# Cross-attention with residual: two heads' exponentials in one tile, two block transposes a quad instead of four

## The chip, the cores and the metric

The kernel runs on one core of a Trainium2 chip. The metric is the device time of one execution in microseconds. Before the change it is 595.76 us, the median of three runs (595.75 to 595.84).

## What is computed

For eight batches of 256 rows by 1024 columns, `x` is layer-normed, multiplied with `Wq` and split into 32 heads of 32 columns. Keys and values are both `ctx_4096` (256 rows a batch), split in the same way. Each head takes the softmax of its 256x256 scores and multiplies the result with the values; the heads are joined, multiplied with `Wout`, and `x` is added. All is fp32.

```python
x = (hidden_states - mu) * jax.lax.rsqrt(var + LN_EPS) * ln_gamma + ln_beta
Q = _split_heads(x @ Wq.T); K = _split_heads(memory_keys); V = _split_heads(memory_values)
scores = jnp.einsum('bhsd,bhtd->bhst', Q, K) * scale
probs = jax.nn.softmax(jnp.where(mask, scores, -jnp.inf), axis=-1)
attn = jnp.einsum('bhst,bhtd->bhsd', probs, V)
return residual + attn.transpose(0, 2, 1, 3).reshape(B, S, HIDDEN) @ Wout.T
```

## The kernel before, in words

**The quad.** The unit of work is a quad: four heads of one batch, which fill the 128 rows of one chunk of Q. There are eight quads a batch and 64 in all, numbered n. One loop runs over n, and the code is issued in the order in which each engine works it off; no scheduler reorders it. In turn n the loop issues, for TensorE: the scores of quad n+1 (`scores`, L362, 16 matmuls into four PSUM banks, one a head), the products of probabilities and values of quad n-2 (`values`, L492), steps of the output projection of the last batch (`product_steps`, L549), the next chunk of Q (`make_q`, L319), and further steps of the projection. For the other engines it issues the softmax of quad n+1 (`softmax_parts`).

**The softmax of one quad.** For each head j, `exps(j)` works on two halves of 128 rows by 256 scores. VectorE (DVE) copies the scores from PSUM to SBUF with the mask added and takes the row's minimum in the same instruction (L396; Q was multiplied with a negative scale); ScalarE (ACT) takes the exponential and sums the row (L400). Then `normalize(j)`: VectorE takes the reciprocal of the two sums (L407), and GpSimd (POOL) multiplies the two halves by it, in place (L409). Then `blocks(j)`: VectorE transposes the head's 128x512 values in blocks of 32x32 into a part of `pT` (L415). `aside` copies a half of `pT` for two heads to `pc` (ScalarE, L421). When all four heads are through, four DMAs on SyncE's queue (L472, L476) exchange blocks of 32 rows between partitions, which ends the transposition. The values of that quad are computed two turns later.

**The order on VectorE.** Within a quad it is: exps 0, 1, 2, reciprocal 0, exps 3, reciprocal 1, transpose 0, reciprocal 2, transpose 1, reciprocal 3, transpose 2, and transpose 3 in `tail()`. In the first nine quads (n up to `NQ`) the tail of a quad is issued behind exps 0 of the next quad; later it follows at once. Into this order other VectorE work is put: `hooks[0]` stands ahead of reciprocal 1 and `hooks[1]` behind transpose 0; a hook is the evacuation of a projection's PSUM bank (`keep`, L561, and `store`, L569). `fill` is a list of pieces of layer norm work of the first quads, of which one piece each was put behind reciprocals 1, 2 and 3 (batch statistics L211, the block transpose L290 of x, `ln_norm`, copies of x's transposes L284). After the quad come the batch statistics (L211 to L216), whose result `ve` GpSimd turns into `rstd` (L217), or the block transposes of x (L290), and GpSimd's sums for the projection (`sum_at`, L539), sums of weights (`sum_wo`, L177), residual additions (`add_res`, L565) and, in the first batch, the folding of gamma into the weights (`fold`, L341 and L342).

**The projection** takes seven products instead of eight per batch, with sums of the operands made by GpSimd. It has one PSUM bank, `po`, so a new product can begin, or go on after a partial result has been taken, only when VectorE or ScalarE has evacuated the bank. `STEPS` sets how many of its 28 steps stand in each turn, ahead of and behind `make_q`. In the last batch, for which no further Q is made, `make_q` falls out and the evacuation is issued ahead of the softmax.

**Buffers.** The pool `ep` of exponentials has four tiles of 128x512, one a head; `ptp` has three `pT`, `ps_s` four banks of scores.

Of the kernel before, what the change touches and what calls it, by code (L numbers as in the profile page):

```python
# [46 lines left out]
F32 = mybir.dt.float32  # L47
# [4 lines left out]
P = 128  # L52
# [7 lines left out]
def xattn_kernel(  # L60
# [13 lines left out]
    T = mask.shape[2]  # L74
# [4 lines left out]
    NS = S // P  # L79
    NT = T // P  # L80
    NO = D // 512
    K = 32
# [11 lines left out]
    vp = ctx.enter_context(tc.tile_pool(name="vp", bufs=2))  # L94
    qp = ctx.enter_context(tc.tile_pool(name="qp", bufs=8))
    atp = ctx.enter_context(tc.tile_pool(name="atp", bufs=2))
    ep = ctx.enter_context(tc.tile_pool(name="ep", bufs=4))
    ptp = ctx.enter_context(tc.tile_pool(name="ptp", bufs=3))
    asp = ctx.enter_context(tc.tile_pool(name="asp", bufs=3))
    up = ctx.enter_context(tc.tile_pool(name="up", bufs=1))  # L100
# [222 lines left out]
    def copy_q(n):  # L323
        b, o = divmod(n, NQ)
        q = qs[n] = qp.tile([P, S + 1], F32, tag="q", name=f"q_{n}")
        if b == 0:
            nc.scalar.activation(q, pqs.pop(n), AF.Copy, scale=NEG_SCALE)  # L327
        elif b == 1:
            nc.scalar.activation(
                q[:, :S], pqs.pop(n), AF.Identity, scale=NEG_SCALE, bias=qb[:, o : o + 1],  # L330
            )
        else:
            nc.scalar.activation(  # L333
                q[:, :S].rearrange("p (s a k) -> p a s k", s=NS, a=NA),
                pqs.pop(n).rearrange("p (a s k) -> p a s k", s=NS, a=NA),
                AF.Identity, scale=NEG_SCALE, bias=qb[:, o : o + 1],
            )
# [29 lines left out]
    def softmax(*args):  # L367
        for _ in softmax_parts(*args):
            pass
# [3 lines left out]
    def softmax_parts(n, new_q=(), between=(), hooks={}, fill=()):  # L373

        fill = list(fill)

        def fill_in():  # L380
            if fill:
                fill.pop(0)()

        pss = scs[n]
        pT = pTs[n] = ptp.tile([P, 2, NI, NH, NS, K], F32, tag="pT", name=f"pT_{n}")
        pc = asp.tile([P, NI, NH, NS, K], F32, tag="pc", name=f"pc_{n}")
        es, mns, dens = {}, {}, {}

        def exps(j, part=range(NS)):
            if 0 in part:  # L390
                es[j] = ep.tile([P, NS, T], F32, tag="e", name=f"e_{n}_{j}")
                mns[j] = sm.tile([P, NS], F32, tag="mn", name=f"mn_{n}_{j}")
                dens[j] = sm.tile([P, NS], F32, tag="den", name=f"den_{n}_{j}")
            e, mn, den = es[j], mns[j], dens[j]
            for s in part:
                nc.vector.tensor_tensor_reduce(  # L396
                    out=e[:, s, :], in0=pss[j][:, s, :], in1=mbs[n // NQ], scale=1.0,
                    scalar=NO_SCORE, op0=ALU.add, op1=ALU.min, accum_out=mn[:, s : s + 1],
                )
                nc.scalar.activation(  # L400
                    e[:, s, :], e[:, s, :], AF.Exp, bias=mn[:, s : s + 1], scale=-1.0,
                    accum_out=den[:, s : s + 1],
                )

        def normalize(j):
            rden = sm.tile([P, NS], F32, tag="rden", name=f"rden_{n}_{j}")
            nc.vector.reciprocal(rden, dens[j])  # L407
            for s in range(NS):
                nc.gpsimd.tensor_scalar(  # L409
                    es[j][:, s, :], es[j][:, s, :], rden[:, s : s + 1], 1.0,  # L410
                    ALU.mult, ALU.mult,
                )

        def blocks(j):
            nc.vector.transpose(  # L415
                pT[:, :, :, j, :, :].rearrange("p a i s k -> p (a i) s k"),
                es[j].rearrange("p s (b t) -> p b s t", t=K),
            )

        def aside(j):  # L420
            nc.scalar.copy(pc[:, :, ts(j, 2)], pT[:, 1, :, ts(j, 2)])  # L421

        if n == 0:
            for j in range(NH - 1):
                exps(j, (0,))
            yield
            exps(NH - 1, (0,))
            fill_in()
            yield
            for j in range(NH):  # L430
                exps(j, (1,))
            normalize(0)
            fill_in()
        else:
            exps(0)
            while tails:
                tails.pop()()
            for done in list(pvs):
                copy_at(done)
            exps(1)  # L440
            exps(2)
            normalize(0)
            exps(3)
        if n <= NQ:
            for q in new_q:
                copy_q(q)
        for hook in hooks.get(0, ()):
            hook()
        normalize(1)
        fill_in()  # L450
        blocks(0)
        for hook in hooks.get(1, ()):
            hook()
        normalize(2)
        fill_in()
        blocks(1)
        aside(0)
        normalize(3)
        fill_in()
        blocks(2)  # L460
        while fill:
            fill_in()
        if n > NQ:
            for q in new_q:
                copy_q(q)

        def tail():
            blocks(3)
            aside(1)

            for r in range(2):
                nc.sync.dma_start(pT[ts(2 * r, K), 1], pT[ts(2 * r + 1, K), 0])  # L472
            for load in between:
                load()
            for r in range(2):
                nc.sync.dma_start(pT[ts(2 * r + 1, K), 0], pc[ts(2 * r, K)])  # L476

        if n < NQ:
            tails.append(tail)
        else:  # L480
            tail()
        yield
# [16 lines left out]
    def copy_at(n):  # L499
        b, c = divmod(n, NQ)  # L500
        if c == 0:
            ats[b] = atp.tile([P, NC, NS, NA, K], F32, tag="at", name=f"at_{b}")
        for r, pv in enumerate(pvs.pop(n)):
            nc.scalar.copy(  # L504
                ats[b][:, c, :, ts(r, 2), :], pv.rearrange("p a s k -> p s a k")
            )
# [86 lines left out]
    for n in range(N):  # L593
        k = min(BATCH0[n] if n < NQ else 1, N - made)
# [56 lines left out]
    for c in range(NC):  # L651
        copy_x0(1, c, nc.scalar if c < NC // 2 else nc.vector)
    first = softmax_parts(0, (1,), (), {}, [
        partial(ln_stats, 1, 0), partial(ln_stats, 1, 1),
        partial(ln_norm, 1, 0, nc.vector), partial(ln_norm, 1, 1, nc.scalar),
# [14 lines left out]
    for n in range(N):  # L670
        b, i = divmod(n - NQ, NQ)
# [6 lines left out]
        if b >= 0 and i in (0, 1, 3, 4):  # L678
            s, h = {0: (0, 0), 1: (1, 0), 3: (1, 1), 4: (0, 1)}[i]
# [147 lines left out]
```

## Time and profile before

| | |
|---|---|
| time before, median of three runs | 595.76 us |
| profiled execution, its own time | 596.43 us |
| its span | 594.6 us |
| L415 transposes of 128x512 | 256, mean 709 ns, 181.4 us busy |
| L409 normalizations of 128x256 | 512, mean 481 ns, 237.3 us busy |
| L396 scores to SBUF with minimum | 512, mean 417 ns, 185.4 us busy |
| L400 exponentials | 512, mean 502 ns, 254.3 us busy |
| L290 transposes of 128x1024 (of x) | 12, mean 1206 ns, 14.5 us busy |
| VectorE waiting for scores (L396 on L362) | 33.5 us |
| VectorE waiting for GpSimd ahead of a transpose | 48.2 us |
| GpSimd waiting for a reciprocal ahead of L409 | 168.7 us |

The profile is of one execution. A row names the line of the kernel, the engine, the operation, the tiles written and read and their shapes, then busy time and mean duration. Where a row has an idle time, it is that of the engine ahead of these instructions, with what ended most of it. Timeline rows begin with the start and the duration in us, and end with the engine's idle time ahead of them where there was some. [...]

### The profile page before, as it was taken

What the parts mean: (1) busy time and instruction counts of PE and PEld (TensorE: products, weight loads), DVE (VectorE), ACT (ScalarE), POOL (GpSimd) and SP (SyncE); (2) the same over time, 40 slices, a digit from 0 to 9 for tenths busy, and PEclk for the clock granted to TensorE, in tenths of its full rate; (3) what the DMA queues carried; (4) which work ended last, traced back from release to release, by engine and by line L of the source; (5) the groups of instructions that cost most, each with busy time, mean ns of one, the idle gap of its engine ahead of it and who ended that gap; (6) DMA issues with size and microseconds to landing.
All of it is one profiled execution on the core that took longest, in us unless ns stands there. A gap on an engine that the chain in (4) does not pass through costs nothing.

```text
span 594.6 us, 18914 instructions
## 1 busy us (share of the span) xinstructions
PE 582.0 (98%) x6680; PEld 389.3 (65%) x6680; DVE 458.3 (77%) x1675; ACT 407.0 (68%) x1380; POOL 347.5 (58%) x630
## 2 busy tenths in 40 slices
PE   9999999999999999999999999999999999999997
PEld 8787776666666676666676667666666667654443
DVE  5878888697887878788787887878787677779801
ACT  4788786776777776686676876677677677667700
POOL 1568896987557644755447653484556564385600
PEclk9999999999999999999999999999999999999999
DMA  8566798545863667544674457654556355466541
GB/s 309 222 165 210 227 255 234 156 114 172 228 185 90 175 177 209 167 113 139 195 225 128 130 157 191 193 155 136 158 145 194 99 162 142 125 181 174 165 126 71
DMA packets 42063, 101.13 MB, mean 170 GB/s; under 512 B 8560, under 2 KB 8560, under 8 KB 41968
## 3 DMA queue, kind: packets, MB, share of 16 engines
q1 hardware_dynamic: 41680, 99.91, 57.4%
q8 instruction: 53, 0.87, 0.7%
q14 instruction: 42, 0.34, 0.2%
q10 hardware_dynamic: 288, 0.01, 0.0%
HBM read 51.65 MB, written 8.39 MB: 101 GB/s over the span
## 4 chain that ended last, share of the span: by engine, by line
PE 76%; POOL 12%; DVE 5%; issue 2%; DMA 2%; ACT 2%; SPq 1%; POOLq 0%; DVEq 0%; ACTq 0%
PE pq L319 29%; PE po_S L549 17%; PE sc L362 9%; PE pv L492 9%; POOL e L409 8%; PE po_A L549 7%; PE po L577 3%; DVE e L396 2%; POOL wo L177 2%; POOL wq L342 1%; PE busy L118 1%; DMA pT<-pc 1%; DVE pT L415 1%; DVE st L211 1%; DMA v<-in_kv_dram 1%
## 5 line engine op out<-in xcount | busy, mean ns | idle before, releaser
L409 POOL TENSOR_SCALAR e<-e,rden 128x256 f32<-128x256 f32 x512 | 237.3, 481 | 172.3 <-DVE rden L407 168.7
L400 ACT ACTIVATE e<-e,mn 128x256 f32<-128x256 f32 x512 | 254.3, 502 | 55.2 <-DVE mn L396 55.2
L319 PE MATMUL pq<-xnT,wq 128*128 128x256 f32 (+1 forms) x1008 | 230.7, 382 | 1.3 <-ACT q L327 1.2
L415 DVE STREAM_TRANSPOSE pT<-e 128x512 f32<-128x512 f32 x256 | 181.4, 709 | 55.4 <-POOL e L409 48.2
L319 PEld LDWEIGHTS pq<-xnT,wq 128*128 128x128 f32 x1008 | 188.9, 190 | 45.1 <-issue 17.9
L396 DVE CUSTOM_DVE_ANT_0 e<-sc,mb 128x256 f32<-128x256 f32 x512 | 185.4, 417 | 33.8 <-PE sc L362 33.5
L421 ACT COPY pc<-pT 128x512 f32<-128x512 f32 x128 | 79.2, 619 | 76.1 <-DVE pT L415 45.3
L549 PE MATMUL po_S<-wo,at 128*128 128x512 f32 x224 | 107.0, 603 | 3.3 <-DVE u L561 1.3
L400 ACT ACTIVATION_READ_ACCUMULATOR e<-e,mn 128x1 f32 x512 | 98.4, 192 | 0.0
L492 PE MATMUL pv<-pT,v 64*32 64x128 f32 x4096 | 74.6, 274 | 2.2 <-DMA pT<-pc 1.4
L362 PEld LDWEIGHTS sc<-k,q 32*128 32x128 f32 x1024 | 46.4, 184 | 46.3 <-issue 23.4
L362 PE MATMUL sc<-k,q 32*128 32x256 f32 x1024 | 74.3, 401 | 0.1
L492 PEld LDWEIGHTS pv<-pT,v 64*32 64x32 f32 x4096 | 57.3, 105 | 25.0 <-issue 12.9
L549 PEld LDWEIGHTS po_S<-wo,at 128*128 128x128 f32 x224 | 40.6, 189 | 38.8 <-issue 31.8
L549 PE MATMUL po_A<-wo,at 128*128 128x512 f32 x112 | 52.0, 598 | 0.0
L407 DVE RECIPROCAL rden<-den 128x2 f32<-128x2 f32 x256 | 39.3, 153 | 9.0 <-ACT e L400 6.3
L396 DVE DVE_READ_ACCUMULATOR2_ANT mn<- 128x1 f32 x512 | 42.7, 83 | 0.0
L549 PEld LDWEIGHTS po_A<-wo,at 128*128 128x128 f32 x112 | 20.8, 190 | 19.1 <-issue 18.4
L217 POOL TENSOR_TENSOR rstd<-ve,mhalf 128x1 f32<-128x1 f32 x16 | 9.4, 585 | 38.8 <-DVE ve L216 38.2
L504 ACT COPY at<-pv 128x128 f32<-128x128 f32 x128 | 26.1, 253 | 8.1 <-PE pv L492 8.1
L333 ACT ACTIVATE q<-pq,qb 128x256 f32<-128x256 f32 x48 | 22.6, 470 | 10.2 <-PE pq L319 10.2
L549 PE MATMUL po_S<-wo,s 128*128 128x512 f32 x56 | 26.9, 605 | 0.6 <-DVE r L569 0.6
(52 smaller groups left out, 299.7 us busy)
## 6 DMA issues: line engine op xcount, KB each, us to landing
v<-in_kv_dram SPq DMA_DIRECT2D x32, 512.0 KB, 4.3
pT<-pT SPq DMA_DIRECT2D x128, 128.0 KB, 2.3
pT<-pc SPq DMA_DIRECT2D x128, 128.0 KB, 3.9
k<-in_kv_dram SPq DMA_DIRECT2D x32, 256.0 KB, 3.4
x<-in_x_dram SPq DMA_DIRECT2D x14, 512.0 KB, 5.6
r<-in_x_dram SPq DMA_DIRECT2D x28, 256.0 KB, 4.4
out_dram<-r SPq DMA_DIRECT2D x28, 256.0 KB, 3.1
xnT<-xe SPq DMA_DIRECT2D x96, 64.0 KB, 3.1
```

Of the source, the lines that this page charges most:

```text
L319: nc.tensor.matmul(pqs[n], wq[:, o, c, :], xnTs[b](c), start=(c == 0), stop=(c == NC - 1),)
L333: nc.scalar.activation(q[:, :S].rearrange("p (s a k) -> p a s k", s=NS, a=NA), pqs.pop(n).rearrange("p (a s k) -> p a s k", s=NS, a=NA), A ...
L362: nc.tensor.matmul(scs[n][j][:, s, :], qs[n][r, ts(s, P)], ks[n - n % 2][r, n % 2, :], start=True, stop=True,)
L396: nc.vector.tensor_tensor_reduce(out=e[:, s, :], in0=pss[j][:, s, :], in1=mbs[n // NQ], scale=1.0, scalar=NO_SCORE, op0=ALU.add, op1=ALU.m ...
L400: nc.scalar.activation(e[:, s, :], e[:, s, :], AF.Exp, bias=mn[:, s : s + 1], scale=-1.0, accum_out=den[:, s : s + 1],)
L407: nc.vector.reciprocal(rden, dens[j])
L409: nc.gpsimd.tensor_scalar(es[j][:, s, :], es[j][:, s, :], rden[:, s : s + 1], 1.0, ALU.mult, ALU.mult,)
L415: nc.vector.transpose(pT[:, :, :, j, :, :].rearrange("p a i s k -> p (a i) s k"), es[j].rearrange("p s (b t) -> p b s t", t=K),)
L421: nc.scalar.copy(pc[:, :, ts(j, 2)], pT[:, 1, :, ts(j, 2)])
L492: nc.tensor.matmul(pvs[n][r][j * HD : (j + 1) * HD], vs[n - n % 2][ts(r, 2 * K), i, ds(n % 2 * P + j * HD, HD)], pT[ts(r, 2 * K), :, i, j, ...
L504: nc.scalar.copy(ats[b][:, c, :, ts(r, 2), :], pv.rearrange("p a s k -> p s a k"))
L549: nc.tensor.matmul(pos[b], operand(b, name)[:, c], wo[:, which, c], start=begins and c == 0, stop=c == NK - 1, skip_group_check=not begins,)
```

## The change

The exponentials of heads 0 and 1 share one tile of 128x1024, and those of heads 2 and 3 another; the pool has two of these instead of four of half the size. `blocks` transposes such a pair with one instruction, and is called twice a quad: `blocks(0)` behind reciprocal 2, `blocks(1)` in the tail. The two calls between reciprocals fall out, and with them two of the places where a piece of `fill` was issued: after the first piece, what is left of `fill` is issued behind reciprocal 3. `hooks[1]` now stands between reciprocals 1 and 2, ahead of the first transpose.

```diff
-    ep = ctx.enter_context(tc.tile_pool(name="ep", bufs=4))
+    ep = ctx.enter_context(tc.tile_pool(name="ep", bufs=2))
...
-        es, mns, dens = {}, {}, {}
+        eps, es, mns, dens = {}, {}, {}, {}
...
-                es[j] = ep.tile([P, NS, T], F32, tag="e", name=f"e_{n}_{j}")
+                if j % 2 == 0:
+                    eps[j // 2] = ep.tile([P, 2, NS, T], F32, tag="e", name=f"e_{n}_{j}")
+                es[j] = eps[j // 2][:, j % 2]
...
         def blocks(j):
             nc.vector.transpose(
-                pT[:, :, :, j, :, :].rearrange("p a i s k -> p (a i) s k"),
-                es[j].rearrange("p s (b t) -> p b s t", t=K),
+                pT[:, :, :, ts(j, 2)].rearrange("p a i j s k -> p (a i) (j s) k"),
+                eps[j].rearrange("p j s (b t) -> p b (j s) t", t=K),
             )
...
         normalize(1)
         fill_in()
-        blocks(0)
         for hook in hooks.get(1, ()):
             hook()
         normalize(2)
-        fill_in()
-        blocks(1)
+        blocks(0)
         aside(0)
         normalize(3)
-        fill_in()
-        blocks(2)
         while fill:
             fill_in()
...
         def tail():
-            blocks(3)
+            blocks(1)
             aside(1)
```

## The prediction

> **What bounds the kernel now.** I read the page's busy shares first, then the stretches, then VectorE's waits, then single quads. The page says that TensorE is never idle for long:
>
> ```profile
> PE 582.0 (98%) x6680; PEld 389.3 (65%) x6680; DVE 458.3 (77%) x1675; ACT 407.0 (68%) x1380; POOL 347.5 (58%) x630
> L409 POOL TENSOR_SCALAR e<-e,rden 128x256 f32<-128x256 f32 x512 | 237.3, 481 | 172.3 <-DVE rden L407 168.7
> L415 DVE STREAM_TRANSPOSE pT<-e 128x512 f32<-128x512 f32 x256 | 181.4, 709 | 55.4 <-POOL e L409 48.2
> ```
>
> Only 12.6 us of the span are idle on TensorE, so relieving VectorE can win little; the question is whether it gets worse. Busy time by stretch (columns: length, then PE, PEld, DVE, ACT, POOL) shows three regimes:
>
> ```profile
> 15.00:125.00 110.00, 106.07 (x1246) 78.81 (x1245) 90.91 (x349) 85.25 (x286) 88.74 (x148) 1.00 0.67 201
> 125.00:527.00 402.00, 401.88 (x4659) 268.35 (x4661) 321.70 (x1173) 285.97 (x974) 231.58 (x428) 1.00 0.56 161
> 527.00:565.00 38.00, 34.51 (x514) 17.60 (x506) 33.91 (x126) 28.24 (x102) 25.18 (x46) 1.00 0.63 182
> ```
>
> TensorE is full in the middle; at the beginning and from 527 us on it waits. In the chain that ended last, those two stretches run through the normalization (POOL e, L409) and VectorE, the middle through TensorE.
>
> I call a quad's exponentials X0 to X3 (L396/L400), its reciprocals R0 to R3 (L407), normalizations N0 to N3 (L409, two instructions each), transposes T0 to T3 (L415). One quad of the last stretch, from the timeline:
>
> ```profile
> 544.62 0.16 DVE L407 RECIPROCAL rden<-den 128x2 f32<-128x2 f32 x1
> 544.87 3.81 POOL L409 TENSOR_SCALAR e<-e,rden 128x256 f32<-128x256 f32 x8 [3.56 <-DVE rden L407]
> 546.75 0.71 DVE L415 STREAM_TRANSPOSE pT<-e 128x512 f32<-128x512 f32 x1
> 547.48 0.17 DVE L407 RECIPROCAL rden<-den 128x2 f32<-128x2 f32 x1
> 547.72 0.71 DVE L415 STREAM_TRANSPOSE pT<-e 128x512 f32<-128x512 f32 x1
> 548.71 0.71 DVE L415 STREAM_TRANSPOSE pT<-e 128x512 f32<-128x512 f32 x1 [0.27 <-POOL e L409]
> 549.35 0.65 DVE L569 TENSOR_TENSOR r<-po_S,r 128x512 f32<-128x512 f32 x1
> 550.05 3.70 PE L549 MATMUL po_S<-wo,s 128*128 128x512 f32 x8 [0.65 <-DVE r L569]
> ```
>
> R0 releases GpSimd, which normalizes eight times without a gap (3.81 us): R3 at 547.48, behind T1, is just in time for N3 at 547.74. N3 ends at 548.68, T3 starts, then the evacuation, and TensorE's next products wait for that. The loop returns every 7.37 us (T3 at 541.35, 548.71).
>
> [...] the kernel already transposes 128x1024 at L290, twelve times, in 1.203 us, against 2 x 0.709 = 1.418. [...]
>
> **The change, part by part.**
>
> Removed and added: 256 transposes of 0.709 us become 128 of, by the L290 row, 1.203: 181.4 to 154 us busy. What counts is start to start: T3 at 340.25 to the next instruction at 340.89 is 0.64; L290 at 332.37 to the next at 333.50 is 1.13. Two became one: 1.28 to 1.13, so 0.3 us saved a quad, 19 us in all, under a full TensorE. The new access pattern isn't in the trace; bounds are one short transpose (0.71) and two (1.42). I take L290's 1.20, as its row has the same element count and minimum and median agree.
>
> Moved: VectorE's order was R1 T0 R2 T1 R3 T2 T3. It is R1 R2 TA R3 TB. TA holds heads 0 and 1 and so waits for N1; R3 is behind TA; N3 waits for R3. TB needs N3.
>
> (a) R3. In a quad as above, N1 ends at 546.72; TA runs from 546.75, R3 follows at 547.89 and takes 0.12, GpSimd starts 0.1 later: N3 at 548.11 instead of 547.74, +0.37. Where GpSimd had been behind (N1 ends 69.66: R3 would come at 70.83, N3 at 71.05, not 70.58) it is +0.47. GpSimd stands still meanwhile.
> (b) TB starts when N3 ends, as T3 did, but holds VectorE for 1.13, not 0.64: +0.5.
> Sum: +0.87 (GpSimd behind: +0.97) before VectorE may go on. Behind TB stand the evacuations, batch statistics, the block transpose of x and the next quad's X0; the ScalarE copy (L421) too.
> (c) Where an evacuation stood between T0 and R2 (three slots in eight), it now stands ahead of TA, and the gap of 0.53 that it made ahead of N2 (L409 x4 ends 337.84, next 338.37) goes: only +0.42 there, and the evacuation comes 0.8 earlier in its quad.
>
> Queues: TensorE's and SP's orders don't change; buffers of e hold as many bytes, and X2 waits only for the last quad's TB, ahead of it on the same engine. In the first quads three pieces of filling work move behind R3: ln_norm's shift (POOL), its x (ACT, 1.24 us) and the second copy of x's transposes.
>
> **Last stretch.** Nothing covers the loop. Five T3s (533.98, 541.35, 548.71, 556.07, 563.44), each 0.87 later: 4.4 us. The work from 565 on is 25.96 of 29.6 us of TensorE, behind them: +4.4.
>
> **Middle.** Per batch of eight slots, from one start of X0 (the rows of 306 to 377 us) to the moment VectorE is free for the next, against the start of the next scores:
> slot 1: needs 8.39, TensorE gives 8.39; 2: 8.99, 9.26; 3: 8.99, 8.39; 4: 8.52, 9.25; 5: 7.95, 8.38; 6: 7.28, 9.25; 7: 7.41, 8.39; 0: 8.49, 9.27.
> Sums: 66.0 of 70.6. The cover is the 4.6 us that VectorE waits for scores in a batch. Added: 0.88 in slots 0, 1, 7; 0.97 in 2; 0.90 in 3; 0.42 in 4, 5, 6: 5.8. It now needs 71.8, 1.2 more than TensorE. VectorE may be late by what its readers leave: in slot 2 the sums on GpSimd, started by ve (L216), end at 319.92 for products at 320.68; in slot 4 the evacuation has some 2 us. After those, each of the four full batches (16th to 47th quad) costs 1.2: +4.8. The batch from quad 48 has no layer norm and waits of 1.2 to 2.4 us a slot: covered.
>
> **Beginning.** Step by step from 12 us: the moved x delays q (L327 24.47) to 25.35: TensorE +0.9. Quads 3 and 4 end +0.6 later each, the next gains a little as its x transposes stop holding R2: +1.9 at scores 66.9. Then GpSimd is the bound (N's, wo 1.25, qb, wq 1.85: a cycle of 6.87): +0.47 per quad by (a), and where ve follows TB, +0.97. From N0 at 67.82 (+1.1, part of the delay being absorbed) I get +1.65, +2.2, +2.95, +3.9, then the sums at 104.2 and TensorE's products at 108.27 by +4.85. Up to the evacuation at 126.54, which gains by (c): +5.3 at 127.3.
>
> Sum: 5.3 + 4.8 + 4.4 = 14.5. The span of 594.6 becomes 609.1; with the 1.8 around it (profiled execution 596.43) 610.9. The median of the runs is 0.7 under the profiled one: 595.76 + 14.5 = **610.3**.
>
> **Rivals.**
> - B: the middle is covered after all. Its excess is 1.2 us of 70.6; errors of 0.15 a slot remove it. Beginning and end remain: +9.7, 605.5. If the beginning is half absorbed too, 603. For it: lateness may spare the ScalarE waits (L407 on e: 6.3).
> - C: the middle is worse. The same error the other way doubles the excess: +4.8, and late copies (L421) may cost the beginning more: 615.
> - D: no change. VectorE only sheds work under a full TensorE, and all lateness is covered: 595.8. Against it: the products at 550.05 wait for the evacuation behind T3, with no cover to use.
> - E: faster. If the long transpose costs hardly more than a short one (below some 0.75 us, where (a) and (b) fall under 0.1 each), quads end no later and evacuations in three slots come 0.8 earlier; TensorE's waits for them (rows of u, r: 3.3) go: 592.5. Against it: L290's minimum of 1.203.
>
> **Numbers.** A 0.50 (606.5 to 614), B 0.25, C 0.17, D 0.04, E 0.04. Two short transposes' length, 1.42, would add 0.3 a quad, up to 12 us; I leave most of that outside. Range 602 to 616. A measurement here can tell 0.2%, 1.2 us, from nothing: faster 0.04, same 0.04, slower 0.92.
>
> **What would show it.** L415: 128 instructions of some 1.20 us. A gap of about 0.4 us ahead of every N3, so L409's idle time behind reciprocals grows by 20 us or more. VectorE's wait for POOL e rises from 48 to over 70 us, its wait for scores (33.5) shrinks towards 10, and TensorE's waits for u, r and the sums grow from about 5 to over 12. The period of the last stretch is 8.24 instead of 7.37. Wrong if: the transpose isn't 1.20; N3 doesn't wait; the middle keeps its 70.6 a batch.

## The result and the profile after

The changed kernel takes 614.12 us (median of six runs, 612.42 to 615.14) against 595.81 us (595.75 to 596.24) for the kernel before. The ratio is 1.0305, with a 95% interval of 1.0291 to 1.0319: slower by 18.3 us. The forecast was 610.3, with a range of 602 to 616. The profiled execution took 613.99 us, with a span of 612.1 us where before it was 594.6.

The page of the kernel after, busy time and the two groups in question; the new lines are L411 for the normalization, L418 for the transpose, L409 for the reciprocal, L398 and L402 for the exponentials:

```profile
PE 589.2 (96%) x6680; PEld 390.0 (64%) x6680; DVE 434.5 (71%) x1547; ACT 405.8 (66%) x1380; POOL 348.4 (57%) x630
L411 POOL TENSOR_SCALAR e<-e,rden 128x256 f32<-128x256 f32 x512 | 238.3, 483 | 184.9 <-DVE rden L409 182.6
L418 DVE STREAM_TRANSPOSE pT<-e 128x1024 f32<-128x1024 f32 x128 | 159.4, 1245 | 83.5 <-POOL e L411 76.7
```

VectorE got what the change offers it: 458.3 us of work became 434.5. TensorE's work didn't change (6680 instructions before and after), but it now stands idle 612.1 - 589.2 = 22.9 us instead of 12.6, and its busy time has grown by 7.2 us as well: by 4.2 in the beginning, 3.0 in the middle and 0.1 at the end, in the stages set out below. The long transpose takes 1.245 us.

Waits of VectorE, before (total us, times, longest):

```profile
DVE pT L415 <- POOL e L409: 48.2, 152, 2.1
DVE e L396 <- PE sc L362: 33.5, 35, 2.7
DVE rden L407 <- ACT e L400: 6.3, 12, 1.7
```

and after:

```profile
DVE pT L418 <- POOL e L411: 76.7, 72, 2.4
DVE rden L409 <- ACT e L402: 42.5, 76, 1.1
DVE e L398 <- PE sc L362: 13.9, 12, 2.5
```

The time that VectorE waited for scores, which was its slack, has shrunk from 33.5 to 13.9 us. In its place it waits for GpSimd and, what the prediction hadn't named, for ScalarE ahead of reciprocals: 42.5 us instead of 6.3. One quad of the last stretch shows both. Timeline after (start, duration, idle time ahead):

```profile
559.24 2.81 POOL L411 TENSOR_SCALAR e<-e,rden 128x256 f32<-128x256 f32 x6 [4.09 <-DVE rden L409]
559.87 0.17 DVE L409 RECIPROCAL rden<-den 128x2 f32<-128x2 f32 x1
560.85 0.17 DVE L409 RECIPROCAL rden<-den 128x2 f32<-128x2 f32 x1 [0.82 <-ACT e L402]
561.13 1.25 DVE L418 STREAM_TRANSPOSE pT<-e 128x1024 f32<-128x1024 f32 x1
562.30 0.12 DVE L409 RECIPROCAL rden<-den 128x2 f32<-128x2 f32 x1
562.51 0.94 POOL L411 TENSOR_SCALAR e<-e,rden 128x256 f32<-128x256 f32 x2 [0.46 <-DVE rden L409]
563.49 1.25 DVE L418 STREAM_TRANSPOSE pT<-e 128x1024 f32<-128x1024 f32 x1 [1.07 <-POOL e L411]
564.65 0.65 DVE L568 TENSOR_TENSOR r<-po_S,r 128x512 f32<-128x512 f32 x1
565.36 1.55 PE L548 MATMUL po_S<-wo,s 128*128 128x512 f32 x3 [1.59 <-DVE r L568]
```

Between R1 (559.87) and R2 (560.85) VectorE is idle 0.82 us, since R2 needs ScalarE's exponential; T0 used to stand there. Then TA, R3 behind it, GpSimd idle 0.46 us, N3, TB, the evacuation, and TensorE waits 1.59 us where before it waited 0.65. TB at 555.18 and 563.49 in the same timeline give a period of 8.31 us; it was 7.37.

To see where the 17.5 us of span arose I use three stages, bounded by two starts of scores (L362, the same two quads in all runs; 129.23 and 526.65 us before): up to the first (beginning), between them (middle), and from the second on (end). The last three columns are differences from the kernel before; every row but "predicted" is one profiled execution.

| kernel | first start | second start | span | beginning | middle | end |
|---|---|---|---|---|---|---|
| before | 129.23 | 526.65 | 594.6 | | | |
| predicted | | | 609.1 | +5.3 | +4.8 | +4.4 |
| after | 136.78 | 539.13 | 612.1 | +7.55 | +4.9 | +5.0 |

TensorE's waits after (those over 2 us):

```profile
PE po_S L548 <- POOL at L538: 4.5, 5, 3.7
PE po_S L548 <- DVE u L560: 3.7, 6, 1.6
PE po_S L548 <- DVE r L568: 3.3, 2, 1.7
PE pq L319 <- ACT q L327: 2.1, 1, 2.1
```

The longest, 3.7 us, is at 115 us, where the products wait for GpSimd's sums. With it the clock granted to TensorE fell from 1.00, full speed, to 0.50. TensorE's timeline, the products before and after, then the work behind the wait for q after:

```profile
108.27 2.84 PE L549 MATMUL po_S<-wo,at 128*128 128x512 f32 x6 [1.00 <-POOL at L539]
114.88 4.34 PE L548 MATMUL po_S<-wo,at 128*128 128x512 f32 x6 [3.74 <-POOL at L538]
25.44 5.43 PE L319 MATMUL pq<-xnT,wq 128*128 128x257 f32 x16 [2.13 <-ACT q L327]
```

Stretches after (length, busy PE, PEld, DVE, ACT, POOL, then the clock, the DMA share and GB/s):

```profile
27.00:29.00 2.00, 2.00 (x6) 1.60 (x5) 0.64 (x6) 2.00 (x9) 1.64 (x4) 0.50 0.42 96
115.00:117.00 2.00, 2.00 (x3) 0.97 (x4) 0.32 (x1) 0.05 (x1) 2.00 (x5) 0.50 0.41 150
119.00:121.00 2.00, 2.00 (x72) 1.50 (x79) 1.93 (x4) 0.69 (x2) 2.00 (x4) 1.00 0.00 0
```

At half clock (0.50) the six products took 4.34 us instead of 2.84, +1.5 us. The same happened at 25 us, behind the 2.1 us wait for q: L319's 16 products took 5.43 us instead of 3.75. These two, 3.2 us, are most of the 4.2 us by which TensorE's busy time grew in the beginning; no term of the prediction held them.

### The profile page after: what moved, and what is told of

It reads as the page before. It is cut to its first block, busy times and chain, and to the rows that moved or that the text cites. A ratio compares the mean times of both kernels' runs of the same rounds, so it can differ in the third digit from the quotient of the medians.

```text
span 612.1 us, 18641 instructions
## 1 busy us (share of the span) xinstructions
PE 589.2 (96%) x6680; PEld 390.0 (64%) x6680; DVE 434.5 (71%) x1547; ACT 405.8 (66%) x1380; POOL 348.4 (57%) x630
## 5 line engine op out<-in xcount | busy, mean ns | idle before, releaser
L411 POOL TENSOR_SCALAR e<-e,rden 128x256 f32<-128x256 f32 x512 | 238.3, 483 | 184.9 <-DVE rden L409 182.6
L402 ACT ACTIVATE e<-e,mn 128x256 f32<-128x256 f32 x512 | 253.8, 501 | 31.1 <-DVE mn L398 31.0
L319 PE MATMUL pq<-xnT,wq 128*128 128x256 f32 (+1 forms) x1008 | 232.4, 384 | 2.9 <-ACT q L327 2.1
L319 PEld LDWEIGHTS pq<-xnT,wq 128*128 128x128 f32 x1008 | 190.0, 191 | 47.5 <-issue 16.6
L418 DVE STREAM_TRANSPOSE pT<-e 128x1024 f32<-128x1024 f32 x128 | 159.4, 1245 | 83.5 <-POOL e L411 76.7
L398 DVE CUSTOM_DVE_ANT_0 e<-sc,mb 128x256 f32<-128x256 f32 x512 | 184.9, 416 | 14.1 <-PE sc L362 13.9
L424 ACT COPY pc<-pT 128x512 f32<-128x512 f32 x128 | 79.1, 618 | 133.6 <-DVE pT L418 76.7
L548 PE MATMUL po_S<-wo,at 128*128 128x512 f32 x224 | 109.7, 616 | 10.4 <-POOL at L538 4.5
L402 ACT ACTIVATION_READ_ACCUMULATOR e<-e,mn 128x1 f32 x512 | 98.0, 191 | 0.0
L362 PEld LDWEIGHTS sc<-k,q 32*128 32x128 f32 x1024 | 47.4, 184 | 47.3 <-issue 28.1
L362 PE MATMUL sc<-k,q 32*128 32x256 f32 x1024 | 76.2, 401 | 0.2
L409 DVE RECIPROCAL rden<-den 128x2 f32<-128x2 f32 x256 | 39.2, 153 | 44.7 <-ACT e L402 42.5
L398 DVE DVE_READ_ACCUMULATOR2_ANT mn<- 128x1 f32 x512 | 42.4, 83 | 0.0
```

Source lines behind the costliest of these rows:

```text
L319: nc.tensor.matmul(pqs[n], wq[:, o, c, :], xnTs[b](c), start=(c == 0), stop=(c == NC - 1),)
L362: nc.tensor.matmul(scs[n][j][:, s, :], qs[n][r, ts(s, P)], ks[n - n % 2][r, n % 2, :], start=True, stop=True,)
L398: nc.vector.tensor_tensor_reduce(out=e[:, s, :], in0=pss[j][:, s, :], in1=mbs[n // NQ], scale=1.0, scalar=NO_SCORE, op0=ALU.add, op1=ALU.m ...
L402: nc.scalar.activation(e[:, s, :], e[:, s, :], AF.Exp, bias=mn[:, s : s + 1], scale=-1.0, accum_out=den[:, s : s + 1],)
L411: nc.gpsimd.tensor_scalar(es[j][:, s, :], es[j][:, s, :], rden[:, s : s + 1], 1.0, ALU.mult, ALU.mult,)
L418: nc.vector.transpose(pT[:, :, :, ts(j, 2)].rearrange("p a i j s k -> p (a i) (j s) k"), eps[j].rearrange("p j s (b t) -> p b (j s) t", t=K),)
```

## The experiments

**What was to be told apart.** My theory was the prediction's: (a) R3 stands behind a transpose and makes N3 late, (b) more is left to transpose when N3 ends. The rivals: that the length of the instruction does it all, or the place does it all; that the middle costs nothing of its own (B); that the two larger buffers do it; that the moved pieces of filling work and the moved evacuations do it.

**Reciprocal 3 first.** The changed kernel with R3 ahead of the first long transpose.

```diff
         normalize(2)
+        normalize(3)
         blocks(0)
         aside(0)
-        normalize(3)
```

> The changed kernel with reciprocal 3 issued ahead of the first long transpose instead of behind it; both transposes stay long. Theory (part a, the late reciprocal, and part b, the longer hold of the second transpose, are two terms of the loss): the gap of about 0.45 us ahead of every last normalization goes, 0.54 us a quad of part b stays. End 5 x 0.54 = 2.7; in the middle a batch needs 66.0 + about 2.7, less than the 70.6 that TensorE gives, so +0; beginning +3, up to +3 more if TensorE's clock drops there again: 602, between 600 and 605. Rival (the length of the instruction alone, or its access pattern, is the cost, wherever the reciprocal stands): stays near 614. Rival (the moved pieces of filling work and hooks are the cost): stays above 608.

Measured 608.16 us (608.04 to 609.5), ratio 1.0212 (1.0195 to 1.0229): only 6 us of the 18 come back, and the forecast was missed. The time even lies just above 608, the bound of the rival that blames filling work and hooks; the run below with the filling moved back answers for the filling, while the moved evacuations were not tested alone. Timeline of a quad of the last stretch in this kernel:

```profile
546.02 3.79 POOL L411 TENSOR_SCALAR e<-e,rden 128x256 f32<-128x256 f32 x8 [1.73 <-DVE rden L409]
547.63 0.17 DVE L409 RECIPROCAL rden<-den 128x2 f32<-128x2 f32 x1 [0.82 <-ACT e L402]
548.61 0.17 DVE L409 RECIPROCAL rden<-den 128x2 f32<-128x2 f32 x1 [0.82 <-ACT e L402]
548.89 2.37 DVE L418 STREAM_TRANSPOSE pT<-e 128x1024 f32<-128x1024 f32 x2
551.18 0.65 DVE L560 TENSOR_TENSOR u<-po_S,p 128x512 f32<-128x512 f32 x1
```

GpSimd's gap is gone (3.79 us in one go), so (a) is as it was described. But R2 and R3 each wait 0.82 us for ScalarE, with nothing to do in between, and both transposes come behind. N3 ends at 549.81 and VectorE is free at 551.18, 1.37 us later; before it was 0.67 (548.68 to 549.35). That is +0.70 a quad, and the period is 8.06 (+0.69; the pair of transposes before it starts at 540.83). I had counted on TA running inside a wait of VectorE, and had not asked what R3 itself waits for.

**Short transposes at the changed places.** The changed kernel, with each long transpose replaced by two short ones at the same place.

```diff
-        blocks(0)
+        block(0)
+        block(1)
         aside(0)
...
-            blocks(1)
+            block(2)
+            block(3)
```

> The changed kernel with its pair tiles and its places of issue, but each long transpose is two short ones again. Theory: the first pair's second transpose ends as early as before, so reciprocal 3 comes in time, and the last transpose is short: end +0, middle +0. Only the moved pieces of filling work of the first quads remain, +0.5 to +0.9, and +1.7 if the wait at 25 us is again followed by a slower TensorE clock: 596.3 to 598.5. Rival (places of issue and shared tiles are the cost): 605 or more.

Measured 601.45 us (600.69 to 603.22), ratio 1.0096 (1.0077 to 1.0115): the place costs more than expected, though less than the rival's 605. The timeline of a quad of the last stretch:

```profile
549.09 0.17 DVE L409 RECIPROCAL rden<-den 128x2 f32<-128x2 f32 x1 [0.82 <-ACT e L402]
549.37 1.30 DVE L424 STREAM_TRANSPOSE pT<-e 128x512 f32<-128x512 f32 x2
550.60 0.12 DVE L409 RECIPROCAL rden<-den 128x2 f32<-128x2 f32 x1
550.82 0.93 POOL L411 TENSOR_SCALAR e<-e,rden 128x256 f32<-128x256 f32 x2 [0.53 <-DVE rden L409]
```

T0 and T1, 1.23 us from 549.37 to R3, delay R3 just as TA does (1.17 us): GpSimd's gap is 0.53 us. The period is 7.83. So (a) is a matter of what was moved, not of what was merged: T0 used to fill VectorE's wait for ScalarE ahead of R2, and T1 the one ahead of R3.

**Only one of the two long.** The kernel of the experiment before, with one pair transposed by the long instruction: first heads 0 and 1, whose edit stands here, then heads 2 and 3.

```diff
+        blocks(0)
-        block(0)
-        block(1)
```

> Only heads 0 and 1 are transposed by a long instruction; heads 2 and 3 by two short ones in the tail. Theory: part a alone, 0.42 to 0.47 us a quad: end +2.1; middle a batch needs some 66.0 + 1.9, covered, +0; beginning +3 and up to 3 more from the clock: 602 to 604. Rival (all of the loss lies in the last transpose): under 598.

> Only heads 2 and 3 are transposed by a long instruction; heads 0 and 1 by two short ones at the place of the first long one. Theory: part b alone, 0.54 us a quad: end +2.7; middle covered, +0; beginning +2 and up to 1.7 from the clock: 600.5 to 602.5. With run of the first pair alone the two parts should not add up to the whole 18.3 us: each is covered in the middle alone, only both together are not (4.8 us of it). Rival (all of the loss is the late reciprocal): under 598.

Measured: first pair long 604.16 us (603.73 to 605.14), ratio 1.0139 (1.0124 to 1.0154), just above its range of 602 to 604; second pair long 609.95 (608.85 to 610.71), ratio 1.0233 (1.0217 to 1.0248), some 8 us above the middle of its forecast, which had assumed that R3 wouldn't be late there. It is (GpSimd's gap is 0.46 to 0.53 us), so this kernel has (a) and (b) both, and its period, 8.36, is close to the 8.31 of the changed one. With the first pair long the period is 7.77.

**The last pair long, the order as before.** To have (b) alone: T0, T1 and the filling at their old places, and TB in place of T2 and T3 (`blocks(1)` is here the changed kernel's, for heads 2 and 3). The exponentials lie in the changed kernel's pair tiles.

```diff
         normalize(3)
         fill_in()
-        blocks(2)
...
-            blocks(3)
+            blocks(1)
```

> The order and the filling of before, transposes of heads 0 and 1 short and at their old places; only heads 2 and 3 are transposed by one long instruction behind N3. This is part (b) alone: R3 is not late. Theory (length and place each have their part): end 5 x 0.54 = +2.7 (period 7.91), middle 66.0 + 8 x 0.5 = 70.0 us of 70.6 a batch, so 0 to +1, beginning +1 to +2: 600 us (598.5 to 602). Rival 1, only the place matters (a reciprocal behind a transpose): 596. Rival 2, the long instruction costs the same wherever the others stand: 610, as in the run with short transposes at the changed place and this long one behind them.

Measured 605.42 us (605.04 to 606.18), ratio 1.0162 (1.0146 to 1.0177), between the rivals and above the theory's range. Timeline:

```profile
543.57 3.80 POOL L411 TENSOR_SCALAR e<-e,rden 128x256 f32<-128x256 f32 x8 [1.62 <-DVE rden L409]
546.17 0.17 DVE L409 RECIPROCAL rden<-den 128x2 f32<-128x2 f32 x1
547.40 1.25 DVE L418 STREAM_TRANSPOSE pT<-e 128x1024 f32<-128x1024 f32 x1 [1.07 <-POOL e L411]
548.57 0.65 DVE L569 TENSOR_TENSOR u<-po_S,p 128x512 f32<-128x512 f32 x1
```

GpSimd has no gap; N3 ends at 547.37, and VectorE idles 1.07 us ahead of it, because T2, which could have run there, is now tied to N3. TB holds VectorE 1.17 us instead of 0.64, and the period is 7.90: +0.53. In the last stretch (a) and (b) are then measured apart, 0.40 to 0.46 and 0.53, and they add up to the 0.94 of the changed kernel. What the theory had too small is the beginning (of its +3.0, 1.6 us are a fall of the clock, shown below) and the middle:

| kernel | first start | second start | span | beginning | middle | end |
|---|---|---|---|---|---|---|
| R3 first | 135.95 | 534.54 | 606.2 | +6.7 | +1.2 | +3.7 |
| short, changed places | 131.17 | 528.40 | 598.9 | +1.9 | -0.2 | +2.5 |
| first pair long | 135.14 | 532.35 | 602.6 | +5.9 | -0.2 | +2.3 |
| second pair long | 134.77 | 535.27 | 608.4 | +5.5 | +3.1 | +5.2 |
| last pair long, old places | 132.24 | 532.18 | 602.8 | +3.0 | +2.5 | +2.7 |
| after | 136.78 | 539.13 | 612.1 | +7.55 | +4.9 | +5.0 |

In the middle, (a) alone is covered and (b) alone costs 0.63 us a batch (2.5 in four), though 8 x 0.53 = 4.2 us is less than the cover of 4.6. I read it so that cover in a slot where TensorE is far behind doesn't help a slot where it is not; that wasn't tested apart.

**Long in the middle alone.** The changed order and both long transposes in quads 16 to 47; the order and the short transposes of before in all others.

```diff
+        long = 2 * NQ <= n < N - 2 * NQ
+        if not long:
+            block(0)
...
+        if long:
+            blocks(0)
+        else:
+            block(1)
...
```

> Long transposes in the changed order only in quads 16 to 47, the order and the short transposes of before in all other quads. Theory (a batch needs 71.8 us on VectorE and GpSimd where TensorE gives 70.6): four batches, +4.8, 600.7 us (599.8 to 601.6), batch period 71.8. Rival (the middle is covered and the losses in it are late beginnings carried on): 596, period 70.6. If slots are worse than summed: 604 or more.

Measured 601.96 us (601.78 to 602.02), ratio 1.0099 (1.0085 to 1.0113), a little above the range of the forecast. The stages are -0.1, +5.0 and 0.0 (starts at 129.17 and 531.59, span 599.6), so it is the middle alone that costs, and four batches cost 1.25 us each. (By the medians the loss is 6.0 us; 0.4 of this lies outside the span, and the median span is 5.6 above that of the kernel before, whose profiled execution was one of its slower ones.) Two starts of scores, one batch apart:

```profile
182.57 1.15 PE L362 MATMUL sc<-k,q 32*128 32x256 f32 x16
254.39 1.15 PE L362 MATMUL sc<-k,q 32*128 32x256 f32 x16
```

The batch takes 71.8 us, as summed, where before it took 70.6, and rival B falls. Where TensorE waits there, from 200 to 500 us in this kernel:

```profile
PE po_S L567 <- DVE u L579: 0.6, 3, 0.2
PE po_S L567 <- POOL at L557: 0.6, 3, 0.2
```

These are the two readers that the prediction named, sums and evacuation, at 0.2 us a time. They show where VectorE is late; of the +5.0 us of the middle, TensorE's idle time holds 2.0, and 3.0 lie in intervals that the records count as busy TensorE.

**A piece of filling work moved back.** The changed kernel with one more call that issues filling work, between R2 and TA. A quad has at most one piece that the change had moved from behind R2 to behind R3, so all of these stand behind R2 again.

```diff
         normalize(2)
+        fill_in()
         blocks(0)
```

> The changed kernel with one more call that issues a piece of layer norm work between reciprocal 2 and the first long transpose, so that the x of the second batch's first half is ready earlier. Theory (the moved piece made TensorE wait 2.13 us for q at 25 us and the granted clock fell after it): the wait is under 1.7 us, L319's 16 products take 3.75 instead of 5.43 us, and some of the 2.6 us so gained lasts: 611.5 us (610 to 613). Rival (the beginning is bound by GpSimd afterwards, what is gained at 25 us is lost again by 105 us): 614.1 within 0.7.

Measured 614.56 us (612.75 to 615.54), ratio 1.0308 (1.0291 to 1.0324): no different from the changed kernel. The forecast was missed, and the rival's time, 614.1, came out; the moved filling is not what costs. The wait for q at 25 us is 1.20 us again, as before, and L319's 16 products take 3.75 us. TensorE's timeline of this kernel:

```profile
24.80 3.75 PE L319 MATMUL pq<-xnT,wq 128*128 128x257 f32 x16 [1.20 <-ACT q L327]
113.22 5.49 PE L549 MATMUL po_S<-wo,at 128*128 128x512 f32 x6 [3.75 <-POOL at L539]
```

The products at 113.22 begin 1.66 us earlier than in the changed kernel (114.88), and then take 5.49 us instead of 4.34, so that they end at 118.7 and 119.2. What was gained at 25 us was thus still there at 113, contrary to the rival's account, which has it lost on GpSimd by then; the longer fall took 1.15 of the 1.66 us. This profiled execution has one fall more near its end, 0.50 from 583.6 to 587.0 us (12 products into `po` take 6.36 us there, 5.31 in the changed kernel), shortly behind an idle time of 1.79 us; in the changed kernel the same wait, 1.78 us, went by without. By the medians the moved filling and the first fall of the clock are worth nothing measurable; how much of that is the other falls stays open.

**Halves.** The opposite of the change: the kernel of before, with T3 cut in two.

```diff
+        def halves(j):
+            for s in range(NS):
+                nc.vector.transpose(
+                    pT[:, :, :, j, s, :].rearrange("p a i k -> p (a i) k"),
+                    es[j][:, s, :].rearrange("p (b t) -> p b t", t=K),
+                )
...
-            blocks(3)
+            halves(3)
```

> The kernel of before with the last head's transpose cut into two instructions of 128x256, the first of which needs only the first half of N3: the opposite of merging. Theory (what VectorE still has to transpose when N3 ends sets the loop): about 0.36 instead of 0.64 us behind N3, so the period of the last stretch is 7.1 instead of 7.37, the end gains 5 x 0.27 = 1.3, the beginning up to 1: 593.6 us (592.8 to 595). Rival (one more instruction a quad costs as much as it frees, or the loop hangs on something else): 595.8 or more.

Measured 593.67 us (593.42 to 594.12), ratio 0.9962 (0.9949 to 0.9974): faster than both kernels, by 2.3 us against the one before, where 593.6 was expected. Timeline of the last stretch:

```profile
542.65 3.81 POOL L409 TENSOR_SCALAR e<-e,rden 128x256 f32<-128x256 f32 x8 [3.29 <-DVE rden L407]
545.51 0.71 DVE L415 STREAM_TRANSPOSE pT<-e 128x512 f32<-128x512 f32 x1
546.14 0.80 DVE L422 STREAM_TRANSPOSE pT<-e 128x256 f32<-128x256 f32 x2
546.86 0.66 DVE L576 TENSOR_TENSOR r<-po_S,r 128x512 f32<-128x512 f32 x1
```

N3 ends at 546.46. The first half started at 546.14, in what was a wait, and VectorE is free at 546.86, 0.40 us behind N3 instead of 0.67. The period is 7.10 instead of 7.37 (T3 halves at 539.04 and 546.14), with one instruction more a quad and VectorE's busy time the same (458.6). The stages are -1.5, -0.2 and -1.3 (starts 127.77 and 524.98, span 591.6).

**Why the beginning reacts so strongly.** At 104 us before, GpSimd waits for `ve`, VectorE's statistics behind the last transpose, before it may make the sums that the products at 108 us need. GpSimd's timeline: before,

```profile
103.70 0.56 POOL L217 TENSOR_TENSOR rstd<-ve,mhalf 128x1 f32<-128x1 f32 x1 [2.43 <-DVE ve L216]
```

with the last pair long at the old places,

```profile
105.70 0.55 POOL L217 TENSOR_TENSOR rstd<-ve,mhalf 128x1 f32<-128x1 f32 x1 [2.96 <-DVE ve L216]
```

and with halves:

```profile
102.51 0.55 POOL L217 TENSOR_TENSOR rstd<-ve,mhalf 128x1 f32<-128x1 f32 x1 [2.17 <-DVE ve L216]
```

The wait is 0.53 longer with TB and 0.26 shorter with halves, the same two amounts as in the last stretch; TensorE's idle time ahead of the products is 1.00 us before, 2.71 with TB, 0.42 with halves, as several such quads add up. With TB the products then took 4.42 us instead of 2.84, with the clock at 0.51 from 110 to 112 us. That made the clock the next question.

**The buffers alone.** Two tiles of 128x1024, all else as before.

```diff
-    ep = ctx.enter_context(tc.tile_pool(name="ep", bufs=4))
+    ep = ctx.enter_context(tc.tile_pool(name="ep", bufs=2))
...
-                es[j] = ep.tile([P, NS, T], F32, tag="e", name=f"e_{n}_{j}")
+                if j % 2 == 0:
+                    eps[j // 2] = ep.tile([P, 2, NS, T], F32, tag="e", name=f"e_{n}_{j}")
+                es[j] = eps[j // 2][:, j % 2]
```

> The kernel of before in everything but the buffers: two exponential tiles of 128x1024 instead of four of 128x512, each head with its short transpose from its half of the tile, at its old place. Theory (order and length of the transposes do it all): as before, 596.0 within 0.7. Rival (two larger buffers come free later, and make the next exponentials wait): 597 or more, with a wait of VectorE ahead of L398 for something else than scores.

Measured 596.48 us (596.23 to 597.32), ratio 1.0011 (1.0005 to 1.0018), as expected and under the rival's bound. The 0.7 us by the medians lie outside the span: its median is 593.9 us, and 594.0 for the kernel before in the same comparison. The buffers are not the cause.

**The clock.** The kernel of before, with GpSimd's first sum of the first projected batch made once or twice more (its result is the same each time), so that TensorE's wait at 108 us grows. GpSimd's work behind the sum comes later by the same time; the transposes and the order are those of before. The code for twice more:

```diff
                 sum_at(b, name)
+                if b == 0 and name == "S1":
+                    for _ in range(2):
+                        nc.gpsimd.tensor_tensor(
+                            operand(b, "S1"), operand(b, "A21"), operand(b, "A22"), ALU.add
+                        )
```

> The kernel of before in which GpSimd makes the first sum of the first projected batch twice (once more, 1.36 us from start to start), ahead of the sum that TensorE waits for at 108 us. TensorE's idle time there becomes 2.36 instead of 1.00 us. If a long idle time lowers the granted clock, 2.04 without and 2.71 with a drop leave this one open; without a drop the 6 products take 2.84 us and the time is 597.4, with it 4.3 to 5.5 and 599.

> The same with the sum made three times: idle 3.72 us. Theory (the idle time lowers the clock, whatever caused it): 6 products take 4.3 to 5.5 us instead of 2.84, and the time is 596.0 + 2.7 + 1.5 to 2.7 = 600.2 to 601.4. Rival (the drop belongs to something else in the changed kernels): 2.84 us, 598.7.

Once more: 597.06 us (596.83 to 598.8), ratio 1.0027 (1.0019 to 1.0035); idle 2.17 us, the products took 2.84 us, no fall in the profiled execution. Of its 15 executions, 11 have a mean granted clock of 1.000 and took 596.83 to 597.39 us, and four have 0.996 or 0.997 and took 598.01 to 598.8. Twice more: 599.91 us (598.65 to 601.12), ratio 1.0062 (1.0041 to 1.0084). TensorE's timeline, once more and twice more, and a stretch of two microseconds of the latter:

```profile
108.99 2.84 PE L549 MATMUL po_S<-wo,at 128*128 128x512 f32 x6 [2.17 <-POOL at L539]
111.05 5.49 PE L549 MATMUL po_S<-wo,at 128*128 128x512 f32 x6 [3.63 <-POOL at L539]
```

```profile
111.00:113.00 2.00, 1.95 (x3) 0.92 (x4) 0.91 (x3) 0.00 (x0) 2.00 (x5) 0.50 0.00 0
```

So the fall needs nothing of the change: here a longer idle time of TensorE, 3.63 us instead of 1.00, brought it. It isn't there in every execution: of the four, two ran with a mean clock of 1.000 and took 598.65 and 598.76 us (the wait alone, 598.7 expected), two with 0.993 and took 601.07 and 601.12 (wait and fall, 600.2 to 601.4 expected). This fall is worth 2.4 us. Without the longer wait it is rare: of 34 executions of the kernel before in this comparison one had a mean clock of 0.997, the others 0.999 or more, while all six of the changed kernel had 0.991 to 0.997.

The granted clock in the falls is 0.50. They last 3.4 us in the changed kernel (25.8 to 29.2 and 114.5 to 117.9) and 6.8, about twice that, with the sum twice more (109.7 to 116.5). The idle time ahead of them differs: with the sum twice more TensorE had been idle for 2.3 us when the clock fell, and there are falls behind idle times of 1.79 us (filling moved back), 2.11 and 2.76 (first pair long) and 2.71 (last pair long) in all, while 2.04 (short, changed places), 2.17 (sum once more) and once 2.81 us went by without one:

```profile
115.36 2.84 PE L548 MATMUL po_S<-wo,at 128*128 128x512 f32 x6 [2.81 <-POOL at L538]
```

This is the kernel with R3 first. It has a fall elsewhere, from 72.7 to 76.1 us (L319's 32 products take 8.11 us there, 7.14 at 54.51); the last idle time over 0.41 us ahead of it, 1.16 us, had ended at 65.22, 7.5 us earlier. So the idle time of TensorE, as the records give it, doesn't settle alone when the clock falls; what else does stays open.

## Why the prediction was right

The time was forecast to 3.8 us, which is a fifth of the loss, and the direction, the mechanism and most of the division into stages held. In the two profiled executions the span grew by 17.5 us where 14.5 were forecast: 2.25 of the missing 3.0 lie in the beginning, 0.6 at the end, 0.1 in the middle. (By the medians 0.8 more are missing: the profiled execution before was 0.6 slower than its median, that after 0.1 faster.) By its own steps:

**(a) R3 behind TA: right, 0.37 forecast.** In the quad shown above, N3 comes 562.51 - 559.24 = 3.27 us after N0 (2.87 before): +0.40. The period with the first pair long alone is +0.40. What the step didn't see is its reason in full. It let T0 and T1 vanish from between the reciprocals at no cost, and the waits for ScalarE that they had filled came into the open: VectorE's wait ahead of reciprocals, 6.3 us, became 42.5. For the sum it didn't matter, for my expectations it did: three of the first four experiments were forecast too fast, R3 first and the two with short T0 and T1 at the place of TA.

**(b) TB holds VectorE longer: right, 0.5 forecast.** It holds it 1.16 to 1.17 us, not 1.13, since the transpose takes 1.245 and not L290's 1.206: +0.53. (TA's hold, 1.17, is longer by as much.)

**(c) The evacuation ahead of TA.** It was not tested alone. The batch of 71.8, in which it is a term, agrees.

**Last stretch: right.** A period of 8.24 was forecast, it is 8.31. The end costs 5.0 instead of 4.4: five times 0.94 instead of 0.87, and 0.3 in the quad ahead of them.

**Middle: right.** 4.8 forecast, 4.9 in the changed kernel and 5.0 where only the middle was changed. That the sum over slots came out exactly is partly luck: with (b) alone the same sum says that nothing is lost (70.2 of 70.6 us), and 0.63 us a batch were measured. Also, with the second pair long the middle costs 3.1 and with both long 4.9, although in the last stretch the two cost the same (periods 8.36 and 8.31). That TA must wait for N1, where T0 needs only N0, would explain it; no run tests that, and it stays open. In the batch from quad 48 VectorE's waits for scores are not all 1.2 to 2.4 us, as read: at 438.73 and 491.66 they are 0.36 and 0.40. It was covered all the same: from its first start of scores to the next batch's it takes 70.5 us after and 70.6 before.

**Beginning: the mis-sized term.** +5.3 was forecast and +7.55 measured. The step that failed is the one on TensorE at 108 us, "then the sums at 104.2 and TensorE's products at 108.27 by +4.85": it moved the products with their old duration. They began 6.6 us later, and took 4.34 us instead of 2.84, behind an idle time of 3.74 us, with the clock at half. Its forerunner is the delay of q at 25 us, given as +0.9: that wait was 2.13 instead of 1.20, as forecast, and 1.7 us of half clock came on top. The quad whose N0 came at 67.82 before, forecast at +1.1, came at +2.5; from there to the products 4.1 us were added, where 3.75 had been summed (GpSimd's gap was 0.51 in these quads, not 0.47). In the run with the filling moved back, which has neither the longer wait nor the fall at 25 us, the same quad came at +0.9, again 4.1 us were added, and the products began at 113.22, +4.95. That this is so near to the +4.85 is partly luck, since the step had held some of the delay of q. The fall behind their wait takes 2.65 there. In the changed kernel's profiled execution the fall at 115 us holds 1.5 of what the beginning lacked; the fall at 25 us and the larger sum make up the rest, less what is absorbed before 136.78. The runs scatter with the clock too: the fastest of the changed kernel, 612.42, had a mean clock of 0.997, the slowest, 615.14, one of 0.991.

**What was to show it.** Hits: 128 instructions; the gap ahead of N3 (0.46); VectorE's wait for POOL e over 70 (76.7); scores near 10 (13.9); the period. Near misses: TensorE's waits for u, r and sums at 11.5 instead of over 12 (before they were 1.3, 1.4 and 1.0, so 3.7 and not "about 5"; rival E's 3.3 for u and r alone should have been 2.7). Miss: L409's idle time behind reciprocals grew by 13.9 us (168.7 to 182.6), not by 20 or more; I read it so that a gap ahead of N3 takes the place of idle time that GpSimd, which isn't the bound, had elsewhere in the quad.

**The rivals.** B (605.5) is refuted by the run with the middle alone, D and E by every run with a long transpose. C's time (615) is near the measured one, but not as C has it: the middle is no worse than forecast, and of what the beginning lost beyond the forecast much is the clock's; late copies were not tested.

## What to carry to other kernels

Before instructions are merged on an engine that isn't the bound, look at what it waits for between them. Here three of the four short ones fitted into waits (ahead of T3 VectorE still stood idle for 0.27 us); the long TB started only when N3 was there, after 1.07 us of idle time, and held the evacuation behind it for 1.16 us. What counted was the time from N3's end to VectorE's being free: 0.67 us before, 1.20 with TB alone, 0.40 with halves, at periods of 7.37, 7.90 and 7.10 us. Where such a time sets a loop, cutting the last instruction is worth a try; here it gained 2.3 us. Where a change makes TensorE wait longer, look at the granted clock too: here waits of 1.79 to 3.75 us had a fall to 0.50 on top, while others of 1.78 to 2.81 us had none.

## What was not expected of the hardware

- The half clock behind idle times of 1.79 to 3.75 us: 0.50 for 3.4 or 6.8 us, worth 1.5 to 2.65 us at six products of 128x512 (2.84 us became 4.34 to 5.49), in some executions and not in others of the same kernel, and once 7.5 us after the last idle time over 0.41 us.
- The transpose of 128x1024 with the pair's access pattern takes 1.245 us, that of x with the same number of elements (L290) 1.206; two of 128x256 take 0.72 us from start to start, one of 128x512 0.64. Cutting it in two costs 0.08 us from start to start.
